# Graph attention on one Trainium2 core: score and self_feat matmuls in 32-column tiles, output blocks of 512 columns

## The chip, the core and the metric

The kernel runs on one core of a Trainium2 chip. Its engines are TensorE (PE, matrix products; its weight loads are shown as PEld), VectorE (DVE), ScalarE (ACT), GpSimd (POOL) and SyncE (SP, which issues most of the DMAs). Each has its own instruction stream and works through it in order; semaphores make one engine wait for another. SBUF is the on-chip memory of 128 partitions. PSUM holds the matmul results: eight banks, each of 512 fp32 values in every partition. The metric is the device time of one execution in microseconds, as the median of several runs. Beside it stands one profiled execution, from which all durations below are taken.

## What is computed

For 16 batches of 512 nodes with 512 features, a condition vector is appended to each node (zero where a node's features sum to zero), and a linear layer makes `self_feat`. Two directions of attention with 16 heads of 32 features are then added to it. Only the first 20 nodes serve as keys and values.

```python
vcq = concat([v, where(v.sum(-1) == 0, 0, q)], -1)
self_feat = vcq @ W_self.T + b_self
output = self_feat
for d in range(2):
    A = (adj if d == 0 else adj.transpose(nodes))[:, :, :20]        # B, N, 20, 11
    bias = A @ w_bias + b_bias
    kv = self_feat[:, :20]
    qh = heads(self_feat @ Wq[d].T + bq[d]); kh = heads(kv @ Wk[d].T + bk[d])
    aff = qh . kh / sqrt(32)                                        # B, N, 16, 20
    aff = where(A.sum(-1) > 0, aff, -9e15) + bias
    w = softmax(aff)
    output += heads(w @ kv) @ Wout[d].T + bout[d]
return v + relu(output)
```

Everything is fp32. The 20 keys of the two directions are handled together, so a node has 16 x 40 = 640 scores.

## The kernel before, in words

The kernel has two parts, a setup and a loop over the 16 batches.

The setup (to about 90 us) folds the key projection and the query weights into one matrix of 608 columns per batch, `g`: 16 heads, two directions and 19 columns, one for each key after the first, as differences from the first key (softmax doesn't change by that). These keys are stored to DRAM in `g_d` and loaded batch by batch (`load_keys`). The query-bias part of the scores goes to `cq_d`. The values with the output weights folded in go to `vw_d` (`values`, L531). In the setup the PE stream is written out by hand: bursts of key matmuls (L566), whose banks ACT (L581) and DVE (L583) empty, and between them pieces of other work after a written plan. The first half batch's mask work stands in that plan too.

In the loop a batch is cut into four tiles of 128 nodes (`nt`). The order of all instructions on each engine is the order of the source; nothing is rescheduled. For each tile:

- `self_feat` (L179) makes the features of the coming nodes, one half of the nodes and two of four feature blocks at a time. Each 128-feature block is made as two matmuls of 64 output partitions (`a`), with weights as the stationary operand and 256 nodes (236 in the first half) as columns. `self_copy` (L199) adds the condition term on DVE and writes `sf` to SBUF.
- `scores` (L246) multiplies `sf` of 64 nodes (stationary, 64 columns of the array) by the keys of eight heads (304 columns). Two such products, `a` = 0 and 1, fill the two halves of the partitions of one PSUM bank: partitions 0 to 63 hold 64 nodes with heads 0 to 7, partitions 64 to 127 the same nodes with heads 8 to 15. Two banks (`g`) take the 128 nodes of a tile.
- Mask and bias: `mask_count` and `mask_mul` (L215, L209) reduce the adjacency of half a batch (two tiles), `mask_add` (L221) combines them into `add`, with nodes on the partitions. Since scores have their nodes in another arrangement, four ACT copies of 64 x 80 (L232) write `both`, in which the partitions are those of the scores. `full_add` (L236) adds the query-bias part `cq`, on POOL.
- Softmax: `weigh` (L258) adds the scores out of PSUM, takes the maximum and subtracts it on DVE (L261, L265, L267), `expo` is one exp on ACT (L272), `normal` (L296) sums and inverts on DVE and multiplies on POOL (L300), and `turn` (L302) transposes in 32 x 32 squares on DVE. `normal` and `turn` of a tile stand one tile later in the order.
- Output: `attend` (L309) is done once for a whole batch, in tile 2 of the next batch, with weights of 32 x 32 from `vd`, so that sixteen such tiles of the array can be in use at once. Four accumulator banks (`ps_acc`, which `self_feat` uses too) hold the four quarters `q` of partitions; for each, `n` picks one of two feature blocks, in 256 columns of a bank. `finish` (L327) adds `sf` on DVE (L331) and applies bias and relu on ACT (L337); `residual` adds `x` on POOL; the next tile stores the result.

The values for `attend` lie in DRAM in `bd_d`, as blocks with zeros around the values of each head. In tile 1 of batch 0, `clear_blocks` (L123) writes the zeros and `blocks` (L136) copies the values from `vw_d` between them, both on SP's queue. `load_values` (L115) then loads each batch's blocks to all four quarters of the partitions. What is issued behind them on SP in batch 0, tile 2, is the load of `x` of batch 2, of the second half of `adj` of batch 1, of `xn` of batch 2, and then of `adj` and `cq` of the next batch.

Also on ACT in tiles 0 and 1 are `row_sum` (L150, for the zero-row test of the next batch), and on DVE `row_mask` (L156), which waits for them; it stands before `normal` and `finish` in DVE's order. For the last batch the outputs are accumulated onto `biased` (self_feat plus bias, L763), which ACT makes in tiles 0 and 1, by an identity matmul (`put_self`, L671), in two parts: three tiles (`most`) and the last one (`rest`).

## Time and profile before

| | |
|---|---|
| median of three runs | 618.52 us (618.28 to 620.65) |
| profiled execution | 617.09 us |
| its span, first to last instruction | 615.2 us |
| mean granted TensorE clock | 0.995 |
| PE busy | 604.0 us, 6828 matmul records |
| DVE busy | 509.3 us |
| ACT busy | 216.2 us |
| POOL busy | 342.4 us |
| DMA traffic | 129.54 MB, mean 211 GB/s |
| one batch in the middle of the loop | 32.5 us: DVE busy 28.92, ACT 12.03, POOL 19.81 |

A line of a group names the source line, the engine, the operation, the tiles written and read, the shape and the count; after the bar stand the time in which the group was busy, the mean duration of one, and the idle time of the engine before it with what ended it. For a matmul, the first shape is contraction rows by array columns (128*64: all 128 rows, 64 columns), then the output. Every fp32 matmul of the source shows as two records, and the mean duration of a record includes its way through the array, so that records overlap and a rate is better read from the distance between starts. A line of the timeline or of the chain gives start and length in us; the count beside it can be a few records short. An instruction that waits in SP's queue holds up what is issued behind it.

### The profile page before, as it was taken

How to read it: one execution, taken by the hardware profiler on the slowest of the kernel's cores; microseconds unless marked ns; L12 is line 12 of the kernel's file. 1: busy time of each engine (PE TensorE's matmuls, PEld its weight loads, DVE VectorE, ACT ScalarE, POOL GpSimd, SP SyncE). 2: the span in 40 equal slices, each digit the busy share in tenths (PEclk: the TensorE clock that was granted, in tenths of full speed). 3: DMA queues.
4: the chain of work that ended last, by engine and by line, in shares of the span. 5: the costliest groups of instructions: out<-in, count | busy, mean ns of one | idle time of the engine just before them, and what ended most of it. 6: DMA issues, size and time to landing. Idle time of an engine off the chain costs nothing.

```text
span 615.2 us, 16426 instructions
## 1 busy us (share of the span) xinstructions
PE 604.0 (98%) x6828; PEld 379.6 (62%) x6828; DVE 509.3 (83%) x818; ACT 216.2 (35%) x480; POOL 342.4 (56%) x269
## 2 busy tenths in 40 slices
PE   9999999999999999999999999999999999999994
PEld 6654558966566656666666666565656665666653
DVE  1586657789888888989898989898988888898995
ACT  1335422233343424342424234343334243434341
POOL 3306332547557474838392938474665747483964
PEclk9999999999999999999999999999999999999998
DMA  8999998719384656738392909292848566674322
GB/s 314 401 394 310 361 370 243 223 72 293 116 233 176 200 210 134 275 90 320 66 343 40 359 18 356 55 326 77 263 147 238 171 187 223 146 265 104 129 71 104
DMA packets 88978, 129.54 MB, mean 211 GB/s; under 512 B 8808, under 2 KB 59016, under 8 KB 86856
## 3 DMA queue, kind: packets, MB, share of 16 engines
q1 hardware_dynamic: 87656, 126.60, 63.1%
q0 software_dynamic: 672, 1.36, 0.9%
q8 instruction: 54, 0.88, 0.6%
q10 hardware_dynamic: 576, 0.53, 0.3%
q14 instruction: 20, 0.16, 0.1%
HBM read 89.90 MB, written 38.93 MB: 209 GB/s over the span
## 4 chain that ended last, share of the span: by engine, by line
PE 95%; DVE 3%; ACT 0%; issue 0%; POOL 0%; DVEq 0%; ACTq 0%; POOLq 0%
PE ps_s L251 42%; PE ps_sf L191 35%; PE ps_o L318 6%; PE ps_v L539 3%; PE ps_k L477 3%; PE ps_kv L428 2%; PE ps_warm L387 1%; DVE o L331 0%; PE ps_nz L174 0%; DVE ps_s L265 0%; DVE sm L298 0%; DVE s L267 0%; DVE full L261 0%; ACT s L272 0%; POOL s L300 0%
## 5 line engine op out<-in xcount | busy, mean ns | idle before, releaser
L251 PE MATMUL ps_s<-g,sf 128*64 128x304 f32 x2048 | 273.7, 420 | 0.5 <-ACT st L581 0.5
L191 PE MATMUL ps_sf<-x,ws_v 128*64 128x256 f32 (+1 forms) x2048 | 222.2, 371 | 0.0
L251 PEld LDWEIGHTS ps_s<-g,sf 128*64 128x64 f32 x2048 | 152.1, 137 | 107.7 <-issue 6.2
L191 PEld LDWEIGHTS ps_sf<-x,ws_v 128*64 128x64 f32 x2048 | 151.4, 137 | 66.5 <-DVE o L331 2.9
L300 POOL TENSOR_TENSOR s<-s,sm 128x640 f32<-128x640 f32 x63 | 80.1, 1272 | 125.3 <-DVE sm L299 116.8
L272 ACT ACTIVATE s<-s 128x640 f32<-128x640 f32 x63 | 46.5, 738 | 197.7 <-DVE s L267 197.7
L241 POOL TENSOR_TENSOR full<-cq,both 128x640 f32<-128x640 f32 x64 | 99.2, 1549 | 24.0 <-ACT both L232 23.5
L213 POOL TENSOR_TENSOR prod<-prod,wb_sb 128x880 f32<-128x880 f32 x32 | 61.3, 1916 | 56.1 <-ACT prod L212 56.1
L340 POOL TENSOR_TENSOR o<-o,x 128x512 f32<-128x512 f32 x60 | 75.5, 1279 | 1.1 <-ACT o L337 1.1
L261 DVE TENSOR_TENSOR full<-ps_s,full 128x608 f32<-128x608 f32 x63 | 49.7, 789 | 26.9 <-PE ps_s L251 20.2
L232 ACT COPY both<-add 64x80 f32<-64x80 f32 x128 | 32.8, 257 | 78.0 <-DVE add L227 76.8
L337 ACT ACTIVATE o<-o,bo 128x512 f32<-128x512 f32 x60 | 40.0, 714 | 44.7 <-DVE o L331 44.7
L298 DVE TENSOR_REDUCE sm<-s 128x32 f32<-128x640 f32 x63 | 51.6, 819 | 4.3 <-ACT s L272 0.9
L265 DVE TENSOR_REDUCE ps_s<-full 128x32 f32<-128x640 f32 x63 | 52.2, 828 | 2.2
L204 DVE SCALAR_TENSOR_TENSOR sf<-nz,qw,ps_sf 128x236 f32<-128x236 f32 (+1 forms) x128 | 52.6, 459 | 1.3 <-PE ps_sf L191 1.1
L267 DVE TENSOR_TENSOR s<-full,ps_s 128x640 f32<-128x640 f32 x63 | 51.7, 821 | 2.2
L307 DVE STREAM_TRANSPOSE wt<-s 128x640 f32<-128x640 f32 x63 | 52.7, 837 | 0.1
L318 PE MATMUL ps_o<-wt,vd 32*32 32x256 f32 (+2 forms) x2176 | 45.7, 372 | 3.1 <-DVE wt L292 1.8
L318 PEld LDWEIGHTS ps_o<-wt,vd 32*32 32x32 f32 x2176 | 30.2, 103 | 18.6 <-issue 7.7
L331 DVE TENSOR_TENSOR o<-ps_o,sf 128x512 f32<-128x512 f32 x60 | 36.4, 669 | 0.2 <-DMA nz_d<-nz 0.2
L218 DVE TENSOR_REDUCE cond<-adj 128x80 f32<-128x880 int32 x32 | 33.2, 1037 | 1.5 <-DMA adj<-in_adj 1.5
L154 ACT ACTIVATE xn<-xn 128x512 f32<-128x512 f32 x56 | 34.3, 613 | 0.0
(213 smaller groups left out, 423.5 us busy)
## 6 DMA issues: line engine op xcount, KB each, us to landing
g<-g_d SPq DMA_DIRECT2D x15, 1216.0 KB, 9.2
g_d<-st SPq DMA_DIRECT2D x16, 1064.0 KB, 6.6
x<-in_xT SPq DMA_DIRECT2D x16, 1024.0 KB, 11.4
out_T<-o SPq DMA_DIRECT2D x60, 256.0 KB, 4.5
xn<-in_xn SPq DMA_DIRECT2D x28, 512.0 KB, 8.7
adj<-in_adj SPq DMA_DIRECT2D x32, 440.0 KB, 7.4
vd<-bd_d SPq DMA_DIRECT2D x64, 128.0 KB, 4.2
nz<-nz_d SPq DMA_DIRECT2D x14, 256.0 KB, 4.6
```

Source lines behind the costliest of these rows:

```text
L191: nc.tensor.matmul(held[0][bass.ts(a, R), i * N // 2 : i * N // 2 + hi - lo], ws_v[:, k, bass.ds((2 * f + i) * P + a * R, R)], xs[b][:, k, ...
L204: nc.vector.scalar_tensor_tensor(sfs[b][:, 2 * f + i, lo:hi], nzs[b][:, lo:hi], qw[:, 2 * f + i, b : b + 1], ps[:, i * N // 2 : i * N // 2 ...
L213: nc.gpsimd.tensor_mul(p, p, wb_sb.unsqueeze(1).to_broadcast([P, 2 * S, L]))
L241: nc.gpsimd.tensor_add(f, cqs[b].unsqueeze(1).to_broadcast(shape), adds[b, nt // 2][:, nt % 2].unsqueeze(2).to_broadcast(shape),)
L251: nc.tensor.matmul(bank[bass.ts(a, R), : WD // 2], sfs[b][:, k, bass.ds(nt * P + g * R, R)], keys[:, k, a], start=(k == 0), stop=(k == C - 1),
L265: nc.vector.tensor_reduce(mx, f, AX.X, ALU.max)
L267: nc.vector.tensor_sub(s, f, mx.unsqueeze(3).to_broadcast(full))
L298: nc.vector.tensor_reduce(sm, s, AX.X, ALU.add)
L300: nc.gpsimd.tensor_mul(s, s, sm.unsqueeze(3).to_broadcast(full))
L307: nc.vector.transpose(wts[b][:, nt], s.rearrange("p a h m -> p (a h m)"))
L318: nc.tensor.matmul(banks[q][bass.ts(e, DH)].rearrange("p (t n) -> p t n", n=32), vds[b][r, e, i, q // 2 * 2 + n], wt[r, :, bass.ts(j, 32)] ...
L340: nc.gpsimd.tensor_add(o[:, c], o[:, c], xs[b][:, c])
```

## The change

The number of partition groups in which scores and self_feat are laid out goes from two to four (`R` from 64 to 32).

- `scores`: 32 nodes are stationary, and four products run side by side, each with four heads (152 columns) on one quarter of the partitions. Two column ranges `j` of a bank take two groups of 32 nodes. `self_feat` makes 32 features per matmul in place of 64.
- `mask_add` arranges the masks for it in sixteen copies of 32 x 80 in place of four of 64 x 80. `load_cq` loads four quarters of the partitions in place of two halves. The views of `full_add` and `weigh` follow, with the same sizes.
- A quarter of the partitions now has the heads that belong to one feature block only, so `attend` needs no `n`: its matmuls have 512 columns (32 nodes from each of sixteen groups), one bank per feature block, and half as many. `finish` and the last batch's code work on contiguous columns.
- `bd_d` has one part per feature block: a batch's load is 128 KB in place of 512 KB. It is cleared as a whole by one DMA (2.1 MB) in place of six DMAs over the zero parts alone (768 KB), and filled by twelve DMAs whose contiguous runs are 128 bytes in place of 512. `values` stores to `vw_d` in the matching order, in runs of 512 bytes in place of 2 KB.

```diff
-    R = P // 2
+    R = P // HL
-    zero = const.tile([32, P], F32, name="zero")
+    zero = const.tile([P, HL * 2 * DH], F32, name="zero")
-    vw_d = dram.tile([2, BM, F], F32, name="vw_d")
-    bd_d = dram.tile([B, 32, HL, 2, C, DH], F32, name="bd_d")
+    vw_d = dram.tile([2, C, BM, P], F32, name="vw_d")
+    bd_d = dram.tile([C, B, 32, HL, 2, DH], F32, name="bd_d")
...
     def load_cq(b):
-        cqs[b] = load.tile([P, H // 2, S], F32, tag="cq", name=f"cq{b}")
-        for a in range(2):
+        cqs[b] = load.tile([P, HL, S], F32, tag="cq", name=f"cq{b}")
+        for a in range(HL):
...
     def load_values(b):
-        vds[b] = gp.tile([P, HL, 2, C, DH], F32, tag="vd", name=f"vd{b}", bufs=1)
-        for q in range(4):
-            nc.sync.dma_start(vds[b][bass.ts(q, 32)], bd_d[b])
+        vds[b] = gp.tile([P, HL, 2, DH], F32, tag="vd", name=f"vd{b}", bufs=1)
+        for c in range(C):
+            nc.sync.dma_start(
+                vds[b][bass.ts(c, 32)].rearrange("p e i g -> p (e i g)"), bd_d[c, b].rearrange("r e i g -> r (e i g)")
+            )
...
     def clear_blocks(zero):
-        for e in range(HL):
-            for i in range(2):
...
+        nc.sync.dma_start(
+            bd_d.rearrange("c b r e i g -> (c b r) (e i g)").rearrange("(n p) w -> p n w", p=P),
+            zero.unsqueeze(1).to_broadcast([P, C * B * 32 // P, HL * 2 * DH]),
+        )

     def blocks():
-        vv = vw_d.rearrange("d (b m) (e w) -> d b m e w", m=NG, e=HL)
+        bb = bd_d.rearrange("c b r e i g -> (c b) r e i g")
+        vv = vw_d.rearrange("d c (b m) (e g) -> d (c b) m e g", m=NG, e=HL)
...
     self_feat:
-                for a in range(2):
+                for a in range(HL):
...
     mask_add:
-        both = adds[b, h] = msk.tile([P, 2, 2, S], F32, tag="both", name=f"both{b}_{h}")
-        for a in range(2):
-            for g in range(2):
+        both = adds[b, h] = msk.tile([P, 2, HL, S], F32, tag="both", name=f"both{b}_{h}")
+        for a in range(HL):
+            for g in range(HL):
                 nc.scalar.copy(
                     both[bass.ts(a, R), :, g], add[bass.ts(g, R)].rearrange("p (t m) -> p t m", t=2)
                 )
...
     def scores(b, nt, g, bank):
-        keys = gs[b].rearrange("p c (a w) -> p c a w", a=2)
-        for k in range(C):
-            for a in range(2):
-                nc.tensor.matmul(
-                    bank[bass.ts(a, R), : WD // 2], sfs[b][:, k, bass.ds(nt * P + g * R, R)], keys[:, k, a],
-                    start=(k == 0), stop=(k == C - 1),
-                )
+        keys = gs[b].rearrange("p c (a w) -> p c a w", a=HL)
+        for j in range(2):
+            for k in range(C):
+                for a in range(HL):
+                    nc.tensor.matmul(
+                        bank[bass.ts(a, R), bass.ts(j, WD // HL)],
+                        sfs[b][:, k, bass.ds(nt * P + (2 * g + j) * R, R)], keys[:, k, a],
+                        start=(k == 0), stop=(k == C - 1),
+                    )
+
+    def softmax_view(f):
+        return f.rearrange("p (a g) h (d m) -> p a (g h d) m", a=2, m=NG)
...
-    def attend(b, n, banks, tiles=slice(0, NT), start=True, stop=True):
-        wt = wts[b][:, tiles].rearrange("p t (g w) -> p (t g) w", g=2)
+    def attend(b, banks, tiles=slice(0, NT), start=True, stop=True):
+        wt = wts[b][:, tiles].rearrange("p t (g w) -> p (t g) w", g=HL)
         for i in range(2):
             for e in range(HL):
-                j = n * HL * S // 32 + e * S // 32 + i
-                for q in range(4):
-                    r = bass.ts(q, 32)
+                j = e * S // 32 + i
+                for a in range(HL):
+                    r = bass.ts(a, R)
                     nc.tensor.matmul(
-                        banks[q][bass.ts(e, DH)].rearrange("p (t n) -> p t n", n=32),
-                        vds[b][r, e, i, q // 2 * 2 + n], wt[r, :, bass.ts(j, 32)],
+                        banks[a][bass.ts(e, DH)].rearrange("p (t n) -> p t n", n=32),
+                        vds[b][r, e, i], wt[r, :, bass.ts(j, 32)],
                         start=start and i == 0, stop=stop and i == 1,
                     )
...
-    def finish(b, o, ns, banks):
-        for q in range(4):
-            c = bass.ds(q // 2 * 2 + ns[0], len(ns))
-            nc.vector.tensor_add(
-                nodes(o[:, c], q % 2), banks[q].rearrange("p (a n) -> p a n", n=32),
-                nodes(sfs[b][:, c], q % 2),
-            )
+    def finish(b, o, banks):
+        for c in range(C):
+            nc.vector.tensor_add(o[:, c], banks[c], sfs[b][:, c])
...
     values:
-                            vw_d[d, bass.ds(t * P, rows)],
-                            v[bass.ds(i * rows, rows)].rearrange("p e c g -> p (e c g)"),
+                            vw_d[d, :, bass.ds(t * P, rows)].rearrange("c r w -> r c w"),
+                            v[bass.ds(i * rows, rows)].rearrange("p (c w) -> p c w", c=C),
```

## The prediction

> **What bounds the kernel now.** I read the page first: TensorE (PE) is busy for 98% of the span at full granted clock, and the chain that ended last lies on two matmul lines.

> ```profile
> PE 604.0 (98%) x6828; PEld 379.6 (62%) x6828; DVE 509.3 (83%) x818; ACT 216.2 (35%) x480; POOL 342.4 (56%) x269
> ...
> PE ps_s L251 42%; PE ps_sf L191 35%; PE ps_o L318 6%; PE ps_v L539 3%; PE ps_k L477 3%; PE ps_kv L428 2%; PE ps_warm L387 1%; DVE o L331 0%; PE ps_nz L174 0%; DVE ps_s L265 0%; DVE sm L298 0%; DVE s L267 0%; DVE full L261 0%; ACT s L272 0%; POOL s L300 0%
> ```

> Then the chain in order of time (start, length, what), in the middle of the run:

> ```profile
> 328.11 2.69 PE ps_o L318 x117
> 330.80 4.24 PE ps_s L251 x32
> 335.04 6.37 PE ps_sf L191 x64
> 341.42 4.09 PE ps_s L251 x32
> 345.51 3.45 PE ps_sf L191 x32
> ```

> A batch takes 32.49 us, and PE has no gap in it. So what counts is the time of matmul streams, and how far the other engines are from making PE wait. For the first, groups by shape and PE's timeline (start, length): one quarter-width row that exists already, and three widths of the output blocks.

> ```profile
> L513 PE MATMUL ps_c<-khD,bqbd 128*32 128x304 f32 x16 | 1.2, 425 | 0.0
> ```

> ```profile
> 328.04 2.76 PE L318 MATMUL ps_o<-wt,vd 32*32 32x256 f32 x128
> ```

> ```profile
> 602.25 2.33 PE L318 MATMUL ps_o<-wt,vd 32*32 32x192 f32 x128 [0.18 <-DVE wt L307]
> ...
> 607.41 1.48 PE L318 MATMUL ps_o<-wt,vd 32*32 32x64 f32 x128 [1.75 <-DVE wt L292]
> ```

> For the second, ScalarE (ACT) and VectorE (DVE) around the output blocks of the same batch:

> ```profile
> 326.81 1.06 ACT L232 COPY both<-add 64x80 f32<-64x80 f32 x4 [1.62 <-DVE add L227]
> 330.84 0.74 ACT L272 ACTIVATE s<-s 128x640 f32<-128x640 f32 x1 [2.97 <-DVE s L267]
> ...
> 332.61 0.18 ACT L154 ACTIVATION_READ_ACCUMULATOR xn<-xn 128x1 f32 x1
> ```

> ```profile
> 330.66 0.84 DVE L307 STREAM_TRANSPOSE wt<-s 128x640 f32<-128x640 f32 x1
> 332.83 0.17 DVE L158 TENSOR_SCALAR nz<-rs 128x4 f32<-128x4 f32 x1 [1.33 <-ACT xn L154]
> 332.91 0.81 DVE L298 TENSOR_REDUCE sm<-s 128x32 f32<-128x640 f32 x1
> 333.76 0.35 DVE L299 RECIPROCAL sm<-sm 128x32 f32<-128x32 f32 x1
> 334.03 2.42 DVE L331 TENSOR_TENSOR o<-ps_o,sf 128x512 f32<-128x512 f32 x4
> ```

> The reader should see a second chain here, nearly as long as PE's. DVE sits idle for 1.33 us until ACT has done exp and two row sums. Only then does it run L331, whose first add (0.63 us) frees the PSUM bank that the next self_feat needs. From the start of the output blocks (328.04) that add ends at 6.61 us and self_feat starts at 6.83 us. PE is later by 0.22 us only.

> **The change part by part.** Each program matmul shows as two records.

> *Scores.* 1024 matmuls of 304 columns become 4096 of 152. Two column tiles run at once: 4.09 us for 16 sets of two is 255.6 ns a set; 236 columns give 199.1 (6.37/32), 256 give 215.6 (3.45/16). That is 0.833 ns a column and 2.3 ns a set. L513's four sets of four tiles start 256 ns apart, so four tiles share a set as two do, and their starts lie 7 ns apart. A tile of nodes then needs 32 sets of 129.0 ns, 4.13 us in place of 4.09: +0.04 us, 64 times, +2.4 us.

> *self_feat.* 1024 matmuls become 2048, four to a set in place of two, the widths stay: 0. Bounds: 0, and 4 us if each added record costs the 2.3 ns of a set.

> [...]

> *Output blocks.* 64 matmuls of 256 columns per batch become 32 of 512, in two rounds of the sixteen array tiles in place of four. The three widths above fit 1.05 us + 6.67 ns a column, i.e. eight passes at 0.833 ns and a fixed part. Streamed columns stay the same (1.71 us). If the fixed part is per round (the rounds start 648, 540 and 327 ns apart for 256, 192 and 64 columns, two passes + 0.216 us each), it falls by 0.43 us; bounds 0 and 0.53 (half). I take 0.43.

> *What is late next.* That gain meets L331. PE would be ready at 6.83 - 0.43 + 0.04 = 6.44 us, but the first add ends at 6.61 and self_feat follows it by 0.055 us (in the one batch where the add was late, it ended at 6.96 and self_feat started at 7.02).

> *The copies of L232* go from 4 to 16 per half batch, 32 partitions each; a copy takes 257 ns, and they start 268 ns apart. I take the same for 32 partitions, as the free size is unchanged. The cover was ACT's idle 2.97 us. Sixteen started at 326.81 occupy ACT until 331.11; exp, now at 330.84, waits in line behind them, 0.27 us later (0.23 against the later end of the scores). The row sums, L158, L298, L299 and L331 queue behind exp: the add ends at 6.84, self_feat starts at 6.90. So of each batch's 0.43 us nothing arrives: +0.07, and +0.11 for the other three tiles' scores, +0.18. In 14 batches: +2.5 us. Without the delay it would be -0.06 a batch.

> *POOL.* The `full` add of L241 also waits for the copies, 3.2 us later, and the residual and normalising multiplies queue behind it. DVE's mask operations L219 and L227 already stretch beside POOL (L219 takes 0.20 to 1.92 us, L227 0.55 to 1.02). Lying differently they can cost DVE 0 to 0.55 us a batch, 0 to 7.7 us in all; most of it meets the 3.6 us of idle DVE in each batch (28.92 of 32.50 us busy), so I take 2.

> *Setup.* The first half batch's copies run at 59.85 to 60.92 us; then ACT empties the key banks (60.92 to 61.94), and the next keys' matmuls start at 62.10, with PE busy until then. Twelve more copies move that to 65.2: +3.1 us (12 x 0.268 = 3.2; bounds 0, if later waits for stores absorb it, and 3.2).

> *Clearing and filling the blocks in DRAM.* All on SP's queue (start, length):

> ```profile
> 95.90 5.74 SPq L131 DMA_DIRECT2D bd_d<-zero  x6
> 101.74 8.93 SPq L147 DMA_DIRECT2D bd_d<-vw_d  x12
> 113.80 1.71 SPq L119 DMA_DIRECT2D vd<-bd_d  x4
> 115.55 0.43 SPq L90 DMA_DIRECT2D x<-in_xT  x1
> 116.03 0.50 SPq L98 DMA_DIRECT2D adj<-in_adj  x1
> ```

> Before them load_cq issues four DMAs for two (+1.1 us). The clear writes 2.1 MB in 2048 runs of 1 KB for 0.77 MB; packets took 30 ns at 512 B and 55 at 1280 B, so 46 ns, 5.9 us on 16 engines, done near 107.3. The first fill now waits for the whole clear: +5.6 us. Behind it on SP stand the other fills, the load of the blocks, x of batch 2, adj of batch 1, xn of batch 2, and adj and cq of the next batch. The fill's 2560 runs of 512 B become 10240 of 128 B. Packets took 11 ns at 44 B, 18 at 256 and 30 at 512: 8 us at 13 ns, 19 us at 30 ns; issuing twelve takes 8 already. So the blocks are complete 4.4 to 16 us later. Loading them is 128 KB a batch for 512 KB (-1.1 us), and SP starts this part behind a queue that the setup's 3 us let drain (-1).

> What waits: adj of batch 1 is issued behind this and lands at 122.51. DVE already idles 1.5 us for it (L218), and PE then stands 1.2 us before batch 0's output blocks, whose fourth bank waits for DVE. So a later adj comes straight onto PE: +2 to +14 us; I take +5, as the issue limit and the 13 ns row lie nearest.

> [...]

> *The end.* Batch 15 has two more activations (L765, 1.34 us) behind its copies: exp moves from 590.99 to 592.6. DVE runs back to back from there to the last sends: +1.6. The last output blocks (64 columns, four rounds of 327 ns) become two of 434: -0.4.

> *Nothing:* L331 and the last adds keep their sizes (contiguous in place of 32-wide runs); `values` stores go from 2 KB to 512 B runs on POOL, 13 us before they are read.

> **Sum.** Scores' first batch and setup +3.2, DRAM blocks +5, fourteen batches +2.5 and +2, end +1.2: +13.9 us, on the profiled execution's 617.09 (span 615.2). The timed median, 618.52, stands 1.4 us above it: 632.

> **The rivals.**

> *Faster.* If L331's first add ended by 6.39 us after the output blocks start (that is the deciding point: exp not held by the copies, and DVE 0.2 us quicker), all 0.43 us would arrive: 15 x 0.43 + 0.4 - 2.4 = -4.5, 614. L331 at 6.61 in thirteen batches speaks against.

> *No change.* The drained queue hides the fill and the stores' waits hide the setup: +2.5 + 1.2 minus a little, 620. L218's idle 1.5 us speaks against.

> *Slow runs in DRAM.* If the fill keeps the overall pace of today's (12 us from 101.7 to 113.7 for 2560 runs, 4.7 ns each), it takes 48 us, 31 more than I have: 663. SP's 0.6 us per issue, whatever its size, explains today's pace better.

> *Quarter tiles pay per matmul.* If the 0.216 us per sixteen matmuls of L318 held for the other two lines, their 6144 matmuls would pay 83 us more: 715. L513 speaks against, but in four sets only.

> **How the numbers follow.** Forecast 0.77 (range of its own 622 to 646, from setup 0 to 3.2, DRAM 2 to 14, POOL 0 to 7.7), slow DRAM runs 0.08, matmul pace 0.06, no change 0.05, faster 0.04. The range 622 to 650 leaves out the last two and most of the 0.14 above. About 0.5% (3.1 us) is what a measurement can tell from no change: faster 0.04, same 0.05, slower 0.91.

> **What would show it.** L232 x512 at some 257 ns; exp waiting for ACT's own queue; self_feat starting 0.055 us behind L331 in every batch; L318 x1088 at some 2.3 us a batch; score tiles at 4.13 us; keys after the first copies 3 us later; adj of batch 1 landing 5 us later and a PE gap of 6 us before the first output blocks. I am wrong if score tiles take over 4.3 us, or if PE shows no gap after 120 us.

## The result, and the profile after

The changed kernel takes 651.64 us (median of four runs, 649.98 to 652.14) where the kernel before takes 618.40 beside it: 1.0524 times as long, with a 95% interval of 1.0493 to 1.0555. The forecast was 632 us in a range of 622 to 650. The direction was right and the size was not: 33.2 us more, where 13.9 had been forecast.

The page of the changed kernel (busy time of the engines; the granted clock in 40 slices of 16.2 us; the mask copies; the queue that brings instructions, with packets, MB and share):

```profile
PE 616.4 (95%) x13932; PEld 470.0 (73%) x13932; DVE 520.7 (80%) x818; ACT 311.8 (48%) x862; POOL 345.2 (53%) x269
...
PEclk9999799987999999999999999999999999999998
...
q8 instruction: 109, 1.79, 1.2%
...
L227 ACT COPY both<-add 32x80 f32<-32x80 f32 x512 | 130.9, 256 | 85.6 <-DVE add L222 80.0
```

The same queue on the page of the kernel before:

```profile
q8 instruction: 54, 0.88, 0.6%
```

TensorE went from 98% to 95% busy, its clock drops in two places, and twice as many instruction packets come in. To see where the 32.9 us of the two spans (615.2 and 648.1) lie, I cut both at the same events of TensorE:

```
stretch                                            before    after    more
start to the first score matmul                     89.83    96.84    +7.0
to the main part of batch 0's output blocks         43.34    52.03    +8.7
to batch 1's output blocks                          32.43    35.50    +3.1
to batch 14's output blocks (13 batches)           422.61   437.01   +14.4
to the end                                          27.00    26.73    -0.3
```

**The setup.** TensorE's timeline of the changed kernel (start, length, what, idle time before it), where the keys wait for ScalarE:

```profile
60.92 1.08 PE L531 MATMUL ps_v<-wo_sb,kvT 128*64 128x512 f32 x4
65.97 0.88 PE L556 MATMUL ps_g(2, 1, 0, 0, 2)0_646<-khD,wq_sb 32*128 32x304 f32 x2 [3.97 <-ACT st L571]
```

ScalarE's own timeline has the reason, the sixteen copies and the bank's eviction behind them:

```profile
60.63 4.26 ACT L227 COPY both<-add 32x80 f32<-32x80 f32 x16 [2.64 <-DVE add L222]
64.91 1.01 ACT L571 ACTIVATE st<-ps_g(2, 0, 0, 1, 2)0_609 128x304 f32<-128x304 f32 x2
```

And the table by stretches (start and end, length, busy time of PE, PEld, DVE, ACT and POOL with their instructions, granted clock, DMA share, GB/s) shows that the pause costs twice:

```profile
66.00:73.00 7.00, 7.00 (x36) 3.68 (x36) 2.35 (x4) 1.00 (x2) 0.00 (x0) 0.53 0.53 200
```

The clock was 0.5 from 65.8 to 72.6 us, so the 3.97 us of idling are followed by 6.6 us of work at half speed (batch 0's sets of four score matmuls start 254 ns apart at a clock of 0.5, from 152.8 to 154.5 us, and 129 to 130 at 1.0 right behind), 3.3 us lost.

**Batch 0.** SyncE's queue (start, length, what), to be held beside the five lines that the prediction shows of the kernel before:

```profile
102.89 2.35 SPq L105 DMA_DIRECT2D cq<-cq_d  x4
105.28 0.43 SPq L125 DMA_DIRECT2D bd_d<-zero  x1
114.10 10.33 SPq L142 DMA_DIRECT2D bd_d<-vw_d  x12
128.35 1.70 SPq L119 DMA_DIRECT2D vd<-bd_d  x4
130.09 1.67 SPq L90 DMA_DIRECT2D x<-in_xT  x1
131.81 0.50 SPq L98 DMA_DIRECT2D adj<-in_adj  x1
```

From the last store of keys to the issue of this adjacency SyncE takes 34.6 us, before 25.8. Of the 8.8 us more, the one clear and the wait for it take 3.0 (105.28 to 114.10, before 95.90 to 101.74), the fills up to the load of the blocks 2.2 (14.2 for 12.1), the query terms 1.2, and that load with x's 1.2; the other 1.1 lie ahead of the query terms. What follows is VectorE's wait for the adjacency, TensorE's wait behind it, and the row of the stretch in the same table:

```profile
138.24 1.07 DVE L213 TENSOR_REDUCE cond<-adj 128x80 f32<-128x880 int32 x1 [10.12 <-DMA adj<-in_adj]
...
145.28 1.99 PE L318 MATMUL ps_o<-wt,vd 32*32 32x512 f32 x6 [6.70 <-DVE wt L307]
148.87 4.03 PE L318 MATMUL ps_o<-wt,vd 32*32 32x512 f32 x58 [1.60 <-issue]
...
138.40:152.80 14.40, 6.10 (x72) 1.42 (x64) 13.25 (x18) 7.31 (x23) 5.06 (x4) 0.59 0.22 81
```

VectorE waits 10.12 us where it had waited 1.5. TensorE then stands for 6.70 us and 1.60 us before the output blocks, and the clock is 0.5 from 140.9 to 154.5.

**The batches.** TensorE's timeline over one of the long batches (34.24 us):

```profile
317.67 2.35 PE L318 MATMUL ps_o<-wt,vd 32*32 32x512 f32 x64
319.95 4.34 PE L247 MATMUL ps_s<-g,sf 128*32 128x152 f32 x128
324.91 6.58 PE L186 MATMUL ps_sf<-x,ws_v 128*32 128x236 f32 x128 [0.61 <-DVE o L327]
331.31 4.32 PE L247 MATMUL ps_s<-g,sf 128*32 128x152 f32 x128
335.44 1.46 PE L186 MATMUL ps_sf<-x,ws_v 128*32 128x256 f32 x20
337.07 2.57 PE L186 MATMUL ps_sf<-x,ws_v 128*32 128x256 f32 x42 [0.17 <-issue]
...
342.65 1.62 PE L247 MATMUL ps_s<-g,sf 128*32 128x152 f32 x42 [0.21 <-issue]
```

The streams are as forecast: output blocks 2.28 us to the next matmul (before 2.69), 4.13 us a tile of scores, sets of four 129.0 ns apart. New are two kinds of waits. One is the bank that L327 frees, which had been foreseen. The other, "issue", waits for nothing that the profile names. The view of the waits adds both up for the weight loads over the whole run (us in total, times, longest); changed kernel first, the kernel before second. "issue" also takes in waits that have nothing to do with instructions, so the kernel before has some of it too:

```profile
PEld ps_s L247 <- issue: 21.6, 30, 1.7
...
PEld ps_sf L186 <- DVE o L327: 8.5, 13, 0.9
```

```profile
PEld ps_s L251 <- issue: 6.2, 15, 0.4
...
PEld ps_sf L191 <- DVE o L331: 2.9, 13, 0.6
```

To size the second kind I took the starts of TensorE's matmuls within one line's stream and summed what exceeds that stream's own spacing by more than 60 ns. In the 13 batches the changed kernel has 20 such gaps, 7.8 us together; the kernel before has none. Counting all records of TensorE from the start (matmuls, weight loads and its waits on semaphores: 28,022; before 13,818), every one of the 20 falls on number 193 or 194 of 256. A packet of the instruction queue is 16,384 bytes, and 28,022 records by 256 are 109 packets, the page's number. After each gap TensorE goes on 1.22 to 1.64 us after the latest packet has come in. So these are waits for instructions: where the kernel before used up a packet in 12.6 us (median), the changed one uses it in 5.2, and at the fastest in 3.9. A single short packet is not enough: in the kernel before about every third one, with output blocks in it, lasts only 2.9 to 6.8 us, between longer ones of 10.9 us or more, and no gap follows.

### The profile page after: what moved, and what is told of

Same layout as the page of the kernel before. It is cut to its first block, busy times and chain, and to the rows that moved or that the text cites. A ratio compares the mean times of both kernels' runs of the same rounds, so it can differ in the third digit from the quotient of the medians.

```text
span 648.1 us, 31041 instructions
## 1 busy us (share of the span) xinstructions
PE 616.4 (95%) x13932; PEld 470.0 (73%) x13932; DVE 520.7 (80%) x818; ACT 311.8 (48%) x862; POOL 345.2 (53%) x269
## 5 line engine op out<-in xcount | busy, mean ns | idle before, releaser
L247 PE MATMUL ps_s<-g,sf 128*32 128x152 f32 x8192 | 286.4, 293 | 4.7 <-issue 3.2
L247 PEld LDWEIGHTS ps_s<-g,sf 128*32 128x32 f32 x8192 | 266.6, 110 | 31.2 <-issue 21.6
L186 PE MATMUL ps_sf<-x,ws_v 128*32 128x236 f32 (+1 forms) x4096 | 228.5, 371 | 5.4 <-DVE o L327 4.5
L186 PEld LDWEIGHTS ps_sf<-x,ws_v 128*32 128x32 f32 x4096 | 146.8, 110 | 71.0 <-DVE o L327 8.5
L227 ACT COPY both<-add 32x80 f32<-32x80 f32 x512 | 130.9, 256 | 85.6 <-DVE add L222 80.0
L300 POOL TENSOR_TENSOR s<-s,sm 128x640 f32<-128x640 f32 x63 | 80.3, 1275 | 61.2 <-DVE sm L299 52.3
L272 ACT ACTIVATE s<-s 128x640 f32<-128x640 f32 x63 | 46.5, 738 | 134.4 <-DVE s L267 133.6
L261 DVE TENSOR_TENSOR full<-ps_s,full 128x608 f32<-128x608 f32 x63 | 49.6, 787 | 24.5 <-PE ps_s L247 19.0
L298 DVE TENSOR_REDUCE sm<-s 128x32 f32<-128x640 f32 x63 | 51.5, 818 | 10.3 <-ACT s L272 8.1
L265 DVE TENSOR_REDUCE ps_s<-full 128x32 f32<-128x640 f32 x63 | 52.2, 828 | 2.2
L267 DVE TENSOR_TENSOR s<-full,ps_s 128x640 f32<-128x640 f32 x63 | 51.7, 821 | 2.2
L318 PE MATMUL ps_o<-wt,vd 32*32 32x512 f32 (+2 forms) x1088 | 42.2, 604 | 11.6 <-DVE wt L307 8.2
L307 DVE STREAM_TRANSPOSE wt<-s 128x640 f32<-128x640 f32 x63 | 52.7, 837 | 0.1
L329 ACT ACTIVATE o<-o,bo 128x512 f32<-128x512 f32 x60 | 38.4, 711 | 28.6 <-DVE o L327 26.8
L213 DVE TENSOR_REDUCE cond<-adj 128x80 f32<-128x880 int32 x32 | 33.2, 1036 | 10.1 <-DMA adj<-in_adj 10.1
L327 DVE TENSOR_TENSOR o<-ps_o,sf 128x512 f32<-128x512 f32 x60 | 36.3, 668 | 0.2 <-issue 0.2
L207 ACT CAST prod<-adj 128x880 f32<-128x880 int32 x32 | 29.2, 912 | 12.1 <-DMA adj<-in_adj 12.0
L318 PEld LDWEIGHTS ps_o<-wt,vd 32*32 32x32 f32 x1088 | 14.3, 105 | 28.3 <-issue 14.9
```

What stands on the lines that cost most here:

```text
L186: nc.tensor.matmul(held[0][bass.ts(a, R), i * N // 2 : i * N // 2 + hi - lo], ws_v[:, k, bass.ds((2 * f + i) * P + a * R, R)], xs[b][:, k, ...
L227: nc.scalar.copy(both[bass.ts(a, R), :, g], add[bass.ts(g, R)].rearrange("p (t m) -> p t m", t=2))
L247: nc.tensor.matmul(bank[bass.ts(a, R), bass.ts(j, WD // HL)], sfs[b][:, k, bass.ds(nt * P + (2 * g + j) * R, R)], keys[:, k, a], start=(k ...
L265: nc.vector.tensor_reduce(mx, f, AX.X, ALU.max)
L267: nc.vector.tensor_sub(s, f, mx.unsqueeze(3).to_broadcast(full))
L300: nc.gpsimd.tensor_mul(s, s, sm.unsqueeze(3).to_broadcast(full))
```

## The experiments

Theory at the start: the 33 us are the setup's pause with its half clock, SyncE's late adjacency with its half clock, and late instruction packets. Each experiment takes one away. Ratios are to the kernel before on the same chip; stretches are those of the table above.

**The old value blocks.** In `clear_blocks`, `blocks` and `values` the code of the kernel before, and in `load_values`:

```diff
-    bd_d = dram.tile([C, B, 32, HL, 2, DH], F32, name="bd_d")
+    bd_d = dram.tile([B, 32, HL, 2, C, DH], F32, name="bd_d")
...
-                vds[b][bass.ts(c, 32)].rearrange("p e i g -> p (e i g)"), bd_d[c, b].rearrange("r e i g -> r (e i g)")
+                vds[b][bass.ts(c, 32)].rearrange("p e i g -> p (e i) g"),
+                bd_d[b, :, :, :, c].rearrange("r e i g -> r (e i) g"),
```

> The changed kernel, but the value blocks in DRAM are laid out, cleared and filled as in the kernel before (runs of 512 bytes, several small clears), and only the loads of the blocks pick one chunk each (runs of 128 bytes). Theory: the one large clear (8.7 us from issue to landing) and the 128-byte fills (14 us for 12) hold up SP and through it the loads behind it; TensorE's 6.7 us of idle time before 145 us goes, and with it the stretch at clock 0.5 from 140.9 to 154.5 us that follows it. Time 640 us (638 to 642): 8.7 + 3.1 less than the changed kernel's 651.6. Rival, the 16 copies of each mask on ScalarE make attend(0) late: 650 to 652, and the idle time stays. Between them, if the loads of 128-byte runs are as slow as the fills were: 645 to 649.

Measured: 649.58 us, ratio 1.0481 (1.0434 to 1.0529). The stretch of batch 0 gave back 4.6 of 8.7 us (47.4), the pause before the output blocks became 2.07 and 2.48 us, and the half clock fell from 13.7 to 6.8 us. But the 13 batches took 442.2 us, 5.2 more. The loads now come in runs of 128 bytes: 5,270 DMA packets on the load queue in 33 us in place of 4,460. The gaps went from 7.8 to 13.0 us, again 17 of 17 at 193 or 194, which is all of the 5.2. So DMA did hold up batch 0, by half of what the theory had said. That the smaller packets make the instructions later is not shown: the gaps are 11.0 us in a run below whose batches load exactly what the changed kernel loads (the clear in the setup), and 12.6 in one without small packets (the first of the last four).

**The first mask's copies on GpSimd.**

```diff
-                nc.scalar.copy(
+                (nc.gpsimd.tensor_copy if (b, h) == (0, 0) else nc.scalar.copy)(
                     both[bass.ts(a, R), :, g], add[bass.ts(g, R)].rearrange("p (t m) -> p t m", t=2)
                 )
```

> The changed kernel, but the 16 copies of the first mask (batch 0, first half, in the setup) run on GpSimd in place of ScalarE. Theory: the 16 copies from 60.6 to 64.9 us put ScalarE's eviction of a key bank, and TensorE behind it, 3.97 us late, and the idle time costs a second time, because TensorE's clock is 0.5 for 6.8 us after it. The first score matmul goes from 96.8 us back to about 90, and the time to 645 us (644 to 647). Rival, only the wait goes and the half clock has another cause: 3 to 4 us less, 648. Rival, GpSimd's copies are late for the first masked sum and the first scores wait there: no gain, 650 to 653.

Measured: 646.31 us, ratio 1.0432 (1.0379 to 1.0484). TensorE's timeline (start, length, what) no longer has the pause:

```profile
61.58 1.08 PE L531 MATMUL ps_v<-wo_sb,kvT 128*64 128x512 f32 x4
62.59 0.53 PE L556 MATMUL ps_g(2, 1, 0, 0, 2)0_646<-khD,wq_sb 32*128 32x304 f32 x2
```

and the stretch after it runs at full clock:

```profile
66.00:73.00 7.00, 7.00 (x100) 3.61 (x96) 4.03 (x8) 3.65 (x7) 5.14 (x5) 1.00 0.82 297
```

The first score matmul came at 90.25 us, 6.6 earlier, from a pause of 3.97. That fits a half clock as the pause's second half. But batch 0 took 3.4 us longer (55.4): TensorE only reached SyncE's late adjacency sooner, and idled 9.29 us there.

**self_feat in 64-column tiles.**

```diff
-                for a in range(HL):
+                for a in range(2):
                     nc.tensor.matmul(
-                        held[0][bass.ts(a, R), i * N // 2 : i * N // 2 + hi - lo],
-                        ws_v[:, k, bass.ds((2 * f + i) * P + a * R, R)], xs[b][:, k, lo:hi],
+                        held[0][bass.ts(a, P // 2), i * N // 2 : i * N // 2 + hi - lo],
+                        ws_v[:, k, bass.ds((2 * f + i) * P + a * (P // 2), P // 2)], xs[b][:, k, lo:hi],
```

> The changed kernel with self_feat in two 64-column tiles as before, scores and output blocks as changed: same output, 4096 fewer records of TensorE (matmuls and weight loads), so about half a packet of 256 instructions less in each batch. Theory, TensorE waits for its instructions where a packet of 16 KB lasts it only 4 to 5 us: the gaps inside self_feat (6, 1.9 us together) go, some of those at the change from scores to self_feat too (13, 5.7 us together with what is not instructions), the 17 gaps inside scores (6.2 us) stay or shift: 648.5 us (647 to 650). Rival, the gaps are not the instruction stream's (a data or semaphore wait that the profile does not show): 651 to 652, gaps unchanged in number and sum. Rival, narrow tiles of self_feat cost stream time: the spacing of self_feat's sets drops, 645 or less.

Measured: 646.77 us, ratio 1.0439 (1.039 to 1.0488). With 93 packets in place of 109 the gaps fell further than expected, from 20 to 3 and from 7.8 to 1.2 us. The 13 batches became only 2.3 us shorter. The other 4.3 went into the changes between streams: from the first matmul of a short self_feat to the next scores takes 3.61 us (3.295 + 0.310) where both have 32-column tiles 3.45 (3.258 + 0.195), and there are six changes between tiles of 32 and 64 columns in a batch. Together they cost more than 4.3 us, and something comes back elsewhere: self_feat starts 6.68 us after the output blocks, in place of 6.90.

**Fewer loads.** From batch 3 on the rows for the flags, the keys and the adjacency of batch 2 are used again, so these batches compute something else.

```diff
-                    if 0 < b < B - 1:
-                        load_keys(b + 1)
+                    if b == 1:
+                        load_keys(2)
+                    elif 0 < b < B - 1:
+                        gs[b + 1] = gs[2]
...
-                    if b + 1 < B:
+                    if b < 2:
                         load_adj(b + 1, 1)
+                    elif b + 1 < B:
+                        adjs[b + 1, 1] = adjs[2, 1]
```

> The changed kernel with most loads of later batches left out: from batch 3 on the rows for the flags, the keys and both halves of the adjacency are those of batch 2 (so the output of those batches is another one); node features, value blocks and stores stay. It moves about 2 MB in a batch where the changed kernel moves 4.8. Theory that the instruction packets come late because they share the DMA engines with these loads: the gaps at one place in the packet of 256 instructions shrink from about 7 us to under 2, time 643 to 646 us. Rival, the packet is asked for too late or takes about 2 us whatever else is under way: gaps stay within a quarter of 7 us, time 650 to 652.

Measured: 644.16 us, ratio 1.0388 (1.0345 to 1.0432). The load queue moved 2.4 MB in 33 us, where the changed kernel moves 5.4. The instructions stayed as they were, 109 packets, and the gaps fell from 20 to 5 and from 7.8 to 2.5 us, the 13 batches by 5.6. The first theory holds: the packets come late because of the other transfers. Two runs at the end repeat this with and without the loads.

**The first bank ahead of the normalisation.** The attend of L714 and the first of its four additions move ahead of `normal(*prev)`:

```diff
+                if nt == 2 and b > 0:
+                    banks = [ps_acc.tile([P, 512], F32, tag="acc", name=f"ps_o{b - 1}_{q}") for q in range(4)]
+                    attend(b - 1, banks)
+                    o = work.tile([P, C, N], F32, tag="o", name=f"o{b - 1}")
+                    nc.vector.tensor_add(o[:, 0], banks[0], sfs[b - 1][:, 0])
                 if prev is not None:
                     normal(*prev)
```

> The changed kernel, but VectorE adds the first of the four output banks (with the attend that fills it) ahead of the normalisation of the tile before, in place of behind it. Theory, in each batch self_feat waits for that bank (it starts 6.90 us after the attend, where the scores before it are done at 6.4 to 6.5), and this wait is where the shorter attend goes: self_feat then starts 6.4 to 6.5 us after the attend, and 14 batches become 0.35 to 0.5 us shorter: 645 to 647 us. Rival, the normalisation that comes 0.7 us later holds up the chain to the next attend, or instruction gaps take the gain: 650 to 653.

Measured: 644.93 us, ratio 1.04 (1.0371 to 1.043). TensorE's timeline of one batch:

```profile
317.26 2.35 PE L318 MATMUL ps_o<-wt,vd 32*32 32x512 f32 x64
319.54 4.34 PE L247 MATMUL ps_s<-g,sf 128*32 128x152 f32 x128
323.70 6.56 PE L186 MATMUL ps_sf<-x,ws_v 128*32 128x236 f32 x128
```

self_feat starts 6.44 us after the output blocks, with no wait. The 13 batches took 432.7 us with 10.6 us of gaps in them, 422.1 without; the changed kernel has 429.2 without its 7.8. So the wait for that bank was worth 7.1 us, if the gaps are simply taken off. That the batches would then be as long as before (422.6) is a subtraction and no run; the last runs below test it.

**The clear in the setup.**

```diff
                 if n == 14:
                     mask_mul(0, 1)
+                    clear_blocks(zero)
...
                     if b == 0:
-                        clear_blocks(zero)
                         blocks()
```

> The changed kernel, but the one large clear of the value blocks is issued late in the setup, some 30 us earlier; the fills stay where they are and need not wait for it. Theory, of the 8.8 us by which SP comes later to the second adjacency of batch 1 (34.6 us after the last store of keys, before: 25.8) the wait for the clear is the largest part, 114.1 - 105.7 = 8.4 us against 5.9 us before for the clears; with no clear there the fills start at about 105.5 us, and the load is issued 8 to 9 us earlier. First score to the main part of attend(0): 43.5 to 45 us (the changed kernel 52.0, before 43.3), no clock of 0.5 behind it, and the time 641 us (639 to 643). Rival, the early clear pushes back the stores of the keys in the setup, or the fills of 128 bytes are as slow as they were and late by themselves: 646 to 650.

Measured: 645.25 us, ratio 1.0415 (1.0386 to 1.0444). SyncE's queue:

```profile
103.94 2.33 SPq L105 DMA_DIRECT2D cq<-cq_d  x4
106.37 11.48 SPq L142 DMA_DIRECT2D bd_d<-vw_d  x12
121.21 1.74 SPq L119 DMA_DIRECT2D vd<-bd_d  x4
122.99 0.43 SPq L90 DMA_DIRECT2D x<-in_xT  x1
123.46 0.50 SPq L98 DMA_DIRECT2D adj<-in_adj  x1
```

The fills start where the theory put them, but from there to the load of the blocks they took 14.8 us by themselves (12.1 before), and the adjacency is issued 29.7 us after the last keys, not at 25.8. Batch 0 took 48.3 us, so 3.7 of 8.7 came back. The half clock is gone in batch 0, where the longest pause is now 1.59 us, as expected. It is gone in the setup too, which was not: the pause of the same kind there was 2.89 us this time, and the first scores came at 93.3 us. The gaps in the batches rose to 11.0 us (440.3). Part of the gain went there.

**Three together.** The edits of the first mask's copies, of the first bank and of the early clear in one kernel, with nothing else changed.

> The changed kernel with the first mask's copies on GpSimd, the clear issued in the setup, and the first output bank added ahead of the normalisation. Theory, the three costs lie one after the other and each returns: the setup 6.6 us (as measured), the wait in batch 0 and the half clock behind it 11 to 12, the batches 5; what is left over the kernel before is the gaps of the instruction stream and the narrower scores, 8 to 11 us: 627 to 630 us. Rival, a part of one cost is the same wait as another's (the copies alone returned 5.3 of 6.6 us): 632 to 638.

Measured: 637.31 us, ratio 1.0284 (1.0256 to 1.0312): the rival's number. Setup 91.1, batches 432.1 (9.1 of them gaps), but batch 0 took 50.2 us and the next stretch 34.6, because the earlier setup again ran into SyncE's fills and a pause of 3.88 us put the clock at 0.5 for 6.8 us.

**More instructions in the kernel before.** There `scores` loops over four pieces of 76 columns, and self_feat over 32-column tiles.

```diff
-        for k in range(C):
-            for a in range(2):
-                nc.tensor.matmul(
-                    bank[bass.ts(a, R), : WD // 2], sfs[b][:, k, bass.ds(nt * P + g * R, R)], keys[:, k, a],
+        for p in range(4):
+            for k in range(C):
+                for a in range(2):
+                    nc.tensor.matmul(
+                        bank[bass.ts(a, R), bass.ts(p, WD // 8)], sfs[b][:, k, bass.ds(nt * P + g * R, R)],
+                        keys[:, k, a, bass.ts(p, WD // 8)],
```

> The kernel before with the same products in more instructions: each matmul of the scores in four pieces of 76 columns, self_feat in tiles of 32 columns; output blocks, fills and masks as before. It has some 24,000 to 30,000 records of TensorE (before 13,818). From 129.0 ns for 152 columns and 255.6 ns for 304 (0.833 ns a column and 2.3 ns a set) the scores would take 0.11 us longer for each tile, 7 us in all, and the changes between tiles of two widths some 4 us (self_feat in 64-column tiles beside scores in 32-column tiles lost that): 629 us without any shortage of instructions. Theory, a packet of 256 instructions then lasts 4 to 5 us, and gaps at one place in the packet (193 or 194 of 256) appear in a kernel that had none, 5 to 12 us together: 634 to 641. Rival, the gaps come from the narrow score tiles or the layout and not from the number of instructions: none there, 627 to 631. Where loading weights for so short a stream becomes the bound, the sets take over 100 ns and the time is over 750 us; then only the gaps' place tells anything.

Measured: 654.14 us (one run). 18 gaps of 7.5 us together, all at 193 or 194, in a layout of the scores that had none; setup and batch 0 have no long pause, and the clock stays at 1.0 until TensorE is done. That more instructions bring the gaps without the new layout is shown, by one run. The rest was sized badly: without gaps the 13 batches are 22 us longer than before, where I had put 11 on the streams of the whole run, so the time is outside both of the expected ranges.

**What is left.** The last four runs close the account. The first has GpSimd's copies, the first bank early, and the value blocks cleared, filled and loaded exactly as before, where the output matmuls take one chunk of the four:

```diff
-                        vds[b][r, e, i], wt[r, :, bass.ts(j, 32)],
+                        vds[b][r, e, i, a], wt[r, :, bass.ts(j, 32)],
```

The second adds the edit of self_feat above to it, the third that of the fewer loads, and the fourth puts the fewer loads into the kernel before.

> The changed kernel with three of its costs taken away: the first mask's copies on GpSimd; the value blocks cleared, filled and loaded in the layout of the kernel before (runs of 512 bytes, of which the output matmuls take one chunk); the first output bank added ahead of the normalisation. Theory, what is left over the kernel before is four loads of the query terms in place of two on SP (about 2.5 us in batch 0) and the gaps of the instruction stream (8 to 11 us in 13 batches): 13 batches of 422.5 us and the gaps, 431 to 433, the time 629 us (626 to 631). Rival, the costs overlap with another that is not named yet: 633 to 637, as with the three parts tried together before.

> The same as the one before, with self_feat in two 64-column tiles: 4096 records of TensorE less. Theory, the gaps fall to 1 to 2 us and the changes between tiles of two widths cost 4 to 5 us in 13 batches: 2 to 5 us less than the one before, 625 us. Rival, gaps stay: no gain.

> The same as the first, with rows, keys and adjacency of later batches left out (from batch 3 on those of batch 2 are used, so the output of those is another one). Theory, the gaps fall to 2 to 3 us: 13 batches in 425 us, time 621 to 623 us, within 0.7% of the kernel before. Rival, the gaps are not from the loads: as the first.

> The kernel before with the same loads left out (rows, keys and adjacency from batch 3 on). Theory, it has no gaps of the instruction stream and its loads are hidden, so it gains nothing: 618 to 620 us, within 0.3% of the kernel before, 13 batches in 422.6 us. Rival, the loads slow something else in any kernel of this shape: 3 to 6 us less, as in the changed kernel, and then its gain there says nothing of instructions.

Measured, in this order: 635.72 us, ratio 1.0268 (1.0234 to 1.0301); 632.73, 1.0205 (1.0181 to 1.0228); 632.20, 1.0207 (1.0187 to 1.0228); and 620.06, 1.0011 (0.9993 to 1.0028).

The last is the control: the kernel before with fewer loads has no gap, its 13 batches take 422.8 us, and it gains nothing. So the 5.6 us that the changed kernel gained by the same cut came from the gaps, not from loads that slow any kernel of this shape.

The first missed its 629 us. Its setup is back (89.9), batch 0 takes 47.0 us (before 43.3), the next stretch 34.7 (pauses of 1.70 and 2.47 us, and a clock of 0.5 for 6.8 us), and the batches 435.3 with 12.6 us of gaps, more than I had put on them. One of its batches has no gap at all and takes 32.23 us, 0.26 less than a batch of the kernel before. That is what the change itself is worth in a batch that nothing disturbs.

The second has one gap of 0.7 us left, and ten of its 13 batches take 33.10 to 33.14 us: the 0.87 above 32.23 is what two tile widths cost a batch, and it eats most of what the gaps gave back. The waits of the weight loads on the instruction stream (us in total, times, longest) of the third, with fewer loads,

```profile
PEld ps_s L252 <- issue: 16.4, 20, 1.7
```

against those of the first

```profile
PEld ps_s L252 <- issue: 24.8, 28, 1.7
```

show the gaps going again (2 are left in the batches, 1.7 us), but the batches still take 429.5 us, 4.5 more than expected. The output blocks of one batch show where the rest went, with fewer loads first, the first of the four second:

```profile
304.39 3.19 PE L323 MATMUL ps_o<-wt,vd 32*32 32x512 f32 x64
```

```profile
304.50 2.35 PE L323 MATMUL ps_o<-wt,vd 32*32 32x512 f32 x64
```

With fewer loads, ten of the 13 batches have longer output blocks, by 7.2 us together. In each of the ten VectorE's second copy of self_feat out of its bank (L204) ends after the output blocks have started, and a matmul of theirs that had been held up, the fourth or the seventh record, starts 0.10 us after that end; in the other three it ends 0.28 us or more before they start, and nothing is held up. Those three batches take 32.23 to 32.24 us again. In the first of the four, the only output blocks held up in this way come right behind its one batch without a gap. So as soon as the gaps are gone, VectorE is next, and 0.26 us a batch is not reached for long: with the gaps taken off, these 13 batches take 427.8 us, 5.2 more than before. None of these kernels is faster than the one before.

## Why the prediction was right in direction and wrong in size

**Scores, self_feat and output blocks: right.** A set of four quarter tiles takes 129.0 ns and a tile of nodes 4.13 us; self_feat's blocks cost 0 to 0.02 us more, forecast 0; the output blocks lose 0.40 us, forecast 0.43. The rival that quarter tiles pay per matmul is out.

**What is late next: right.** The whole gain went into L327's first bank. self_feat starts at 6.895 us after the output blocks, forecast 6.90, and with the bank freed early at 6.44, the number that the prediction gave for TensorE alone. This was the condition of the faster rival. Moving the addition met it, the batches shortened by the 0.5 us each (gaps taken off), and the kernel was still 4% slower, so the condition was right and not sufficient.

**POOL's 2 us and the end's 1.2: not found.** The effect that the prediction feared for POOL is there, and larger than its bound: VectorE's mask operations beside POOL became 13.1 us longer over the run (L214 23.2 us for 13.3, L222 27.1 for 23.9), where it allowed 7.7. But this met idle time of VectorE, and no wait of TensorE on GpSimd appears in the batches. In one batch (at 486.8 us) a longer L222 made the first bank 0.3 us late. Exp of the last tile was late by 1.9 us, and the last stretch is still 0.3 us shorter than before.

**Setup: mis-sized.** Forecast 3.1 us, measured 7.0. The step "move that to 65.2: +3.1 us" counted the wait alone, which came out at 3.97. What failed is that it stopped there: the clock was 0.5 for 6.83 us behind this pause. No pause of the kernel before is over 1.75 us long, and its clock was 0.5 only once TensorE was done, so its trace had no row for this, and the prediction set no bound for it either.

**Clearing and filling: mis-sized.** "I take +5" within 2 to 14. SyncE came 8.8 us later, TensorE 8.7, and 3.1 more in half clock behind it. The clear cost 3.0, forecast 5.6. Two terms of the sum failed: the time that the drained queue would give back (-1) did not come, and the load with x's became 1.2 us longer, not 1.1 shorter. The fills were near the low end: 14.2 us for 10,240 runs of 128 bytes, against 12.1 for 2,560 of 512, so the rival of slow runs in DRAM (31 us more) is out. A packet of 128 bytes took 13 ns (median), the number that it had assumed, and one of 512 bytes 27. The half clock behind the pause is the term that is missing here too.

**The batches: a term was missing.** Forecast 2.5 in fourteen batches (and POOL's 2); measured 14.4 in thirteen. Of these, -3.4 is the undisturbed batch (13 x 0.26), 6.8 the pauses for the bank (13 of 0.54 to 0.91 us, less 0.11 where nothing is waited for), 7.8 the gaps; 3.2 is left in smaller pauses at the changes between streams, which I did not resolve. The step that failed is "four to a set in place of two, the widths stay: 0" for self_feat, with its like for scores: it priced a record by the time that TensorE takes for it, and not by what it takes to bring it. The prediction itself makes 4096 matmuls of 1024 for the scores and 2048 of 1024 for self_feat (the pages have 13,932 matmul records for 6,828), and the page of the kernel before has the row that would have asked the question, 54 packets of 16 KB in a queue of their own.

Together: 7.0 + 8.7 + 3.1 + 14.4 - 0.3 = 32.9. About 6.1 of it is half clock (3.3 and 2.8), 7.8 or more is instructions.

## What to carry to other kernels

Count instructions as traffic: divide the records of the busiest engine by a packet's 256 (here 28,022 records and 109 packets) and by the time of its streams, and ask whether the next packet can come in so soon beside the loads of that stretch; here a stream of 12.6 us a packet was safe, with single ones of 3 us in it, and one of 5.2 us throughout was not. A pause of TensorE is not priced by its length alone (here one of 3.97 us had 6.83 us at a clock of 0.5 behind it): look up what the clock did after pauses like it. And a gain of one engine arrives only as far as the next wait allows, so look for the wait that was 0.2 us short of mattering, and for the one behind it: the bank that L327 frees was covered by TensorE's own work before, and the bank that L204 frees by the gaps.

## What the runs showed of the hardware

**Instructions compete with data.** The same 109 packets cost 7.8 us of gaps beside 5.4 MB of loads in 33 us and 2.5 us beside 2.4 MB; in the pair of the last runs 12.6 us and 1.7. With all the loads the sum differs from kernel to kernel (7.8 to 13.0 us, one profile each), and what sets it was not found. The time of a packet itself hardly changes (median 1.0 to 1.1 us in all of them), and TensorE goes on 1.2 to 1.65 us after it in every gap of nine kernels. So what is late is its start, as far as these traces show. Whether the request or its turn on the DMA engines is late was not tried.

**A change of tile width costs some 0.1 us.** Between streams of one tile width the second starts where the next set of the first would have: 0.209 us after the last matmul of self_feat with 64-column tiles on both sides, 0.195 with 32 on both (sets of 215.6 ns). From 64 columns to 32 it was 0.310. From scores in 32 columns to self_feat it was 0.110 us with 32 and 0.223 with 64.
